# Convolution stage: the copies into column order issued on ScalarE instead of GpSimd, and two tap matrices instead of three in one half of the channels

## The chip, the cores and the metric

The kernel runs on one core of a Trainium2 chip. The metric is the device time of one execution in microseconds, as the median of several executions. Before the change three executions took 19363.97, 19373.8 and 19378.93 us, median 19373.8.

## The reference

The model has four layers on an image of 2 x 128 x 128 pixels with 128 channels in float32. Only the beginning of the last layer matters here:

```python
xz = x @ W_in.T                               # 128 -> 512 channels, x is group-normalised
xc, z = jnp.split(xz, 2, axis=-1)             # 256 channels each
xc = conv_general_dilated(xc, conv_w, (1, 1), ((1, 1), (1, 1)),
                          feature_group_count=256) + conv_b      # 3 x 3, depthwise
xc = silu(xc)
x1 = _local_scan(xc, Hh, Ww, 32, 32)                      # windows of 32 x 32, row order
x2 = _local_scan(xc, Hh, Ww, 32, 32, column_first=True)   # the same windows, column order
x3, x4 = x1 and x2 reversed
# selective scans of x1 .. x4, layer norm, gate with silu(z), output projection
```

So each of the 256 channels is a projection of the 128 inputs, followed by a 3 x 3 filter of its own (nine taps), a bias and a silu. The scans then need every window of 32 x 32 pixels in row order and in column order.

## The kernel before

`program` (L1705) runs the layers one after the other: `layer0`, `layer1`, `layer2`, and for the last layer `layer3_conv` (L1092), `layer3_scan` (L1216) and `layer3_out` (L1624). Between the parts of the last layer the data goes through tensors in DRAM. `layer3_conv` fills `xs` (each window in row order, `xs[0]`, and in column order, `xs[1]`, with channels on the partitions) and `xst` (each window with pixels on the partitions). `layer3_scan` reads them.

`layer3_conv` works on strips of 32 rows: two images (`b`) times four strips (`hg`), eight in all. In each strip:

- `xpad` (two buffers) is the normalised input of 34 rows by 130 columns. It is loaded in pieces `x3l` on SP's queue (L1138) and normalised by ScalarE (L1142); GpSimd clears the border (L1127 to L1132).
- For each half `e` of the 256 channels, TensorE multiplies `xpad` with the projection `win` into `zps` (L1157) and ScalarE copies it to `xz` (L1161, three buffers), whose side columns GpSimd clears (L1152, L1153).
- The strip is cut into four groups `g` of eight rows. A tap of the filter can be computed in two ways. As a matrix, TensorE multiplies `xpad`, shifted by the tap, with `cw`, which is the projection times the tap's weight, and sums the taps in PSUM in `cps` (L1170, two buffers). As a vector operation, VectorE multiplies the shifted `xz` with the weight in `cv` and adds it to `acc` (L1179, three buffers). Its first operation for a group adds to `cps`, the others add to `acc` itself. Taps 0 to 2 (`MAT`) are matrices, taps 3 to 8 (`VEC`) are vector operations, in both halves. So VectorE has six operations of 128 x 1024 per group, 384 in the stage. A matrix costs two matmuls per group, each of which leaves two records in the trace.
- ScalarE applies bias and silu to `acc` and writes `xw` (L1183, three buffers), which holds the four windows of the strip one after the other.
- For each window `wg`, GpSimd copies `xw` in column order to `xv` (L1192, two buffers, one half of the channels per copy): it reads with a step of 32 elements and writes without gaps. SP's queue stores `xw` (L1193) and `xv` (L1196). TensorE transposes `xw` in blocks of 128 x 128 into `xtps` (L1205, two buffers), ScalarE copies these to `xt` (L1210, two buffers), and SP's queue stores it to `xst` (L1213).

[...] In this stage the order isn't written out by hand: a scheduler interleaves the work of neighbouring groups, halves and strips on each engine, within the limits of the buffers and dependencies. In the scan the order is held as written (`in_order`, L114). [...]

Of the kernel before, what the change touches and what calls it, by code (L numbers as in the profile page):

```python
# [9 lines left out]
F32 = mybir.dt.float32  # L10
AF = mybir.ActivationFunctionType
ALU = mybir.AluOpType
# [3 lines left out]
P = 128  # L16
# [6 lines left out]
def cols_of(handle, n, offset=0):  # L23

    return bass.AP(handle.tensor, handle.offset + offset, [[1, P], [P, n // P]])


def rows_of(handle, n, offset=0):

    return bass.AP(handle.tensor, handle.offset + offset, [[0, P], [1, n]])  # L30
# [1061 lines left out]
def layer3_conv(tc, cs, ins, x3, xs, xst, sc, sh):  # L1092

    nc = tc.nc  # L1100
    MAT = (0, 1, 2)
    VEC = (3, 4, 5, 6, 7, 8)
    with ExitStack() as ctx:
        pool = lambda name, bufs, **kw: ctx.enter_context(tc.tile_pool(name=name, bufs=bufs, **kw))
        w = pool("l3a_w", 1)
        two = pool("l3a_two", 2)
        three = pool("l3a_three", 3)
        ps_t = pool("l3a_ps_t", 2, space=PSUM)
        ps_z = pool("l3a_ps_z", 2, space=PSUM)
        ps_c = pool("l3a_ps_c", 2, space=PSUM)  # L1110
        win = w.tile([P, 256], F32, name="win")
        nc.sync.dma_start(win, ins["winT"][:, 0:256])

        cw = w.tile([P, len(MAT), 256], F32, name="cw")
        nc.sync.dma_start(cw.rearrange("p t e -> p (t e)"), rows_of(ins["conv_w_t"], len(MAT) * 256))

        cv = w.tile([P, 9, 2], F32, name="cv")
        nc.sync.dma_start(cv.rearrange("p t e -> p (t e)"), cols_of(ins["conv_w_t"], 9 * 256))
        cb = w.tile([P, 2], F32, name="cb")
        nc.sync.dma_start(cb, cols_of(ins["L3_conv_conv_b"], 256))  # L1120
        nc.vector.tensor_tensor(
            cw, cw, win.unsqueeze(1).to_broadcast([P, len(MAT), 256]), ALU.mult
        )
        for b in range(NB):
            for hg in range(4):
                xpad = two.tile([P, 34, 130], F32, name=f"xpad_{b}_{hg}", tag="xpad")
                nc.gpsimd.memset(xpad[:, :, 0:1], 0.0)  # L1127
                nc.gpsimd.memset(xpad[:, :, 129:130], 0.0)
                if hg == 0:
                    nc.gpsimd.memset(xpad[:, 0:1, 1:129], 0.0)  # L1130
                if hg == 3:
                    nc.gpsimd.memset(xpad[:, 33:34, 1:129], 0.0)  # L1132
                r = max(32 * hg - 1, 0)
                end = min(32 * hg + 33, HW)
                while r < end:
                    n = min(8, end - r)
                    xl = two.tile([P, 8, HW], F32, name=f"x3l_{b}_{hg}_{r}", tag="x3l")
                    nc.sync.dma_start(  # L1138
                        xl[:, 0:n, :].rearrange("c r w -> c (r w)"), x3[b, :, r * HW : (r + n) * HW]
                    )  # L1140
                    p0 = r - 32 * hg + 1
                    nc.scalar.activation(  # L1142
                        xpad[:, p0 : p0 + n, 1:129], xl[:, 0:n, :], AF.Identity,
                        bias=sh[:, b : b + 1], scale=sc[:, b : b + 1],
                    )
                    r += n
                xw = []
                for e in range(2):
                    t = f"{b}_{hg}_{e}"
                    ep = slice(e * P, (e + 1) * P)  # L1150
                    xz = three.tile([P, 34, 130], F32, name=f"xz_{t}", tag="xz")
                    nc.gpsimd.memset(xz[:, :, 0:1], 0.0)  # L1152
                    nc.gpsimd.memset(xz[:, :, 129:130], 0.0)  # L1153
                    for r in range(0, 34, 4):
                        n = min(4, 34 - r)
                        zps = ps_z.tile([P, 4, HW], F32, name=f"zps_{t}_{r}", tag="zps")
                        nc.tensor.matmul(  # L1157
                            zps[:, 0:n, :], win[:, ep], xpad[:, r : r + n, 1:129],
                            start=True, stop=True,
                        )  # L1160
                        nc.scalar.copy(xz[:, r : r + n, 1:129], zps[:, 0:n, :])  # L1161
                    xwe = three.tile([P, 4, 32, 32], F32, name=f"xw_{t}", tag="xw")
                    xw.append(xwe)
                    for g in range(4):
                        cps = ps_c.tile([P, 8, HW], F32, name=f"cps_{t}_{g}", tag="cps")
                        for i, tap in enumerate(MAT):
                            dy, dx = tap // 3, tap % 3
                            for h in range(2):
                                r = 8 * g + 4 * h + dy
                                nc.tensor.matmul(  # L1170
                                    cps[:, 4 * h : 4 * h + 4, :], cw[:, i, ep],
                                    xpad[:, r : r + 4, dx : dx + HW],
                                    start=(i == 0), stop=(i == len(MAT) - 1),
                                )
                        acc = three.tile([P, 8, HW], F32, name=f"acc_{t}_{g}", tag="acc")
                        for i, tap in enumerate(VEC):
                            dy, dx = tap // 3, tap % 3
                            r = 8 * g + dy
                            nc.vector.scalar_tensor_tensor(  # L1179
                                acc, xz[:, r : r + 8, dx : dx + HW], cv[:, tap, e : e + 1],  # L1180
                                cps if i == 0 else acc, ALU.mult, ALU.add,
                            )
                        nc.scalar.activation(  # L1183
                            xwe[:, :, 8 * g : 8 * g + 8, :].rearrange("p g r w -> p r g w"),
                            acc.rearrange("p r (g w) -> p r g w", w=32),
                            AF.Silu, bias=cb[:, e : e + 1],
                        )
                for wg in range(4):
                    t = f"{b}_{hg}_{wg}"
                    xv = two.tile([P, 2, 32, 32], F32, name=f"xv_{t}", tag="xv")  # L1190
                    for e in range(2):
                        nc.gpsimd.tensor_copy(xv[:, e], xw[e][:, wg].rearrange("p h w -> p w h"))  # L1192
                        nc.sync.dma_start(  # L1193
                            xs[0, b, hg, wg, :, e, :], xw[e][:, wg].rearrange("p h w -> p (h w)")
                        )
                        nc.sync.dma_start(  # L1196
                            xs[1, b, hg, wg, :, e, :], xv[:, e].rearrange("p w h -> p (w h)")
                        )
                    xt = two.tile([P, 8, 256], F32, name=f"xt_{t}", tag="xt")
                    for g in range(4):  # L1200
                        tps = ps_t.tile([P, 2, 2, P], F32, name=f"xtps_{t}_{g}", tag="x3t")
                        for j in range(2):
                            for e in range(2):
                                h0 = 4 * (2 * g + j)
                                nc.tensor.transpose(  # L1205
                                    tps[:, j, e, :],
                                    xw[e][:, wg, h0 : h0 + 4, :].rearrange("p h w -> p (h w)"),
                                    cs.ident,
                                )
                        nc.scalar.copy(  # L1210
                            xt[:, 2 * g : 2 * g + 2, :], tps.rearrange("p j e d -> p j (e d)")
                        )
                    nc.sync.dma_start(xst[b, hg, wg].rearrange("(t p) d -> p t d", p=P), xt)  # L1213
# [603 lines left out]
```

## Time and profile before

| what | value |
| --- | --- |
| median of three executions | 19373.8 us |
| the profiled execution, whole | 19390.22 us |
| its span | 19388.3 us |
| convolution: VectorE's first operation of L1179 starts | 6059.55 us |
| its last starts | 6636.2 us |
| first VectorE operation of the scan's preparation | 6674.98 us |
| first operation of the scan itself (L1579) | 6707.10 us |
| VectorE busy over the span | 16402.8 us (85%) |
| ScalarE busy | 14886.8 us (77%) |
| TensorE busy | 14890.7 us (77%) |
| GpSimd busy | 12448.3 us (64%) |

A row of the group view gives the source line, the engine, the operation, the tiles written and read, shape and count, then the busy time in us, the mean duration of one operation in ns, and the engine's idle time just before these operations with what ended it. A row of the timeline gives start and length in us of a run of like operations. In it, a bracket is idle time ahead of the run and what ended it. PE is TensorE's matmul, PEld its weight load, DVE VectorE, ACT ScalarE, POOL GpSimd, SP the engine that issues the DMAs. A table of windows gives for each stretch its length, the busy time of each engine with the count of operations, the clock granted to TensorE, the mean busy share of the DMA engines and GB/s.

Most of the span is the scan, which starts after the convolution. The convolution takes about 3% of it.

### The profile page before, as it was taken

To read this page: it belongs to the slowest core of one execution; us is meant where nothing else is said; L and a number is where in the kernel's file an instruction comes from. 1 tells how busy PE (TensorE), PEld (TensorE's weight loads), DVE (VectorE), ACT (ScalarE), POOL (GpSimd) and SP (SyncE) were. 2 spreads that over 40 slices of the span, in tenths; PEclk is the share of its full clock that TensorE was granted. 3 is DMA by queue.
4 is the path that set the end of the run, shared out by engine and by line. 5 is a ranking of instruction groups with operands and counts; after the bars stand their busy time and mean duration, and the time that the engine had idled before them with its cause. 6 is when DMAs were issued, how large, how long until landed. Compare 5 with 4: busy or idle time off the path is not lost. (4 is left out here: it accounts for less than half of the span.)

```text
span 19388.3 us, 284041 instructions
## 1 busy us (share of the span) xinstructions
PE 14890.7 (77%) x100346; PEld 8797.9 (45%) x100346; DVE 16402.8 (85%) x20891; ACT 14886.8 (77%) x30269; POOL 12448.3 (64%) x6909
## 2 busy tenths in 40 slices
PE   7888888886446777777777777777777777777756
PEld 5665666663113344444444444444444444444445
DVE  6666666336668899999999999999999999999977
ACT  4665666333333499999999999999999999999932
POOL 0000000110001399999999999999999999999954
PEclk9999999887778898999899999999999999999977
DMA  2000000221113444444444444444444444444455
GB/s 48 23 22 22 17 17 14 70 64 50 38 38 118 168 118 113 117 113 117 111 119 115 116 115 116 120 111 120 112 120 111 120 110 121 115 115 116 114 177 182
DMA packets 1302045, 1861.84 MB, mean 96 GB/s; under 512 B 120269, under 2 KB 685517, under 8 KB 1298318
## 3 DMA queue, kind: packets, MB, share of 16 engines
q1 hardware_dynamic: 1264638, 1834.44, 36.1%
q8 instruction: 797, 13.06, 0.3%
q10 hardware_dynamic: 35984, 9.22, 0.2%
q14 instruction: 626, 5.13, 0.1%
HBM read 1398.74 MB, written 444.60 MB: 95 GB/s over the span
## 5 line engine op out<-in xcount | busy, mean ns | idle before, releaser
L1579 DVE TENSOR_TENSOR_SCAN hs<-da,state,ups 128x512 f32<-128x512 f32 x8192 | 9924.2, 1260 | 349.9 <-PE ups L1571 285.0
L1597 POOL TENSOR_TENSOR hs<-hs,cb 128x2048 f32<-128x2048 f32 x2048 | 9389.2, 4585 | 432.0 <-ACT state L1591 185.4
L1571 PE MATMUL ups<-ident,but 128*128 128x128 f32 x32768 | 5595.9, 302 | 2547.1 <-DVE hs L1579 1650.1
L1571 PEld LDWEIGHTS ups<-ident,but 128*128 128x128 f32 x32768 | 3882.8, 151 | 6164.1 <-DVE hs L1579 3512.0
L1536 ACT ACTIVATE but<-du,bt 128x256 f32<-128x256 f32 x12800 | 5330.1, 498 | 4.8 <-DVE du L1434 4.2
L1512 ACT ACTIVATE da<-db,na 128x512 f32<-128x512 f32 x8192 | 5226.5, 711 | 24.3 <-DMA db<-dd 19.9
L1550 PE MATMUL yps<-hs,sel 128*32 128x512 f32 x16384 | 2504.1, 687 | 31.5 <-POOL hs L1597 12.6
L1531 POOL TENSOR_TENSOR but<-du,bt 128x256 f32<-128x256 f32 x3584 | 2161.8, 625 | 17.9 <-issue 17.9
L282 POOL TENSOR_TENSOR xres<-xres,rowb 128x256 f32<-128x256 f32 x128 | 93.4, 730 | 2645.4 <-DMA xres<-in_x 2536.3
L390 ACT COPY pT<-tps 128x512 f32<-128x512 f32 x1280 | 724.6, 587 | 1121.0 <-PE tps L385 1121.0
L385 PE MATMUL tps<-ident,s 128*128 128x128 f32 x8192 | 1179.6, 283 | 367.9 <-DVE pT L388 273.4
L358 DVE CUSTOM_DVE_ANT_0 s<-sps,relbias 128x512 f32<-128x512 f32 x2048 | 1321.3, 683 | 113.5 <-PE sps L342 108.0
L385 PEld LDWEIGHTS tps<-ident,s 128*128 128x128 f32 x8192 | 888.0, 142 | 898.4 <-issue 485.6
L370 ACT ACTIVATE s<-s,nm 128x1024 f32<-128x1024 f32 x1024 | 1163.5, 1137 | 85.0 <-DVE nm L368 81.6
L1127 POOL MEMSET xpad<- 128x34 f32 x8 | 1.3, 165 | 1577.8 <-PE xs L1021 1503.0
L342 PE MATMUL sps<-kc,qT 32*128 32x512 f32 x4096 | 595.0, 648 | 0.8 <-DVE nm L358 0.8
L1591 ACT COPY state<-hs 128x4 f32<-128x4 f32 x2048 | 381.1, 186 | 264.3 <-DVE hs L1579 264.3
L388 DVE COPY pT<-tps 128x512 f32<-128x512 f32 x768 | 526.8, 686 | 55.2 <-PE tps L385 54.6
L1317 PE MATMUL xdps<-xc,xpw 128*40 128x512 f32 x1024 | 541.7, 611 | 15.0 <-DMA xpw<-in_x_projT 15.0
L1349 PE MATMUL dtps<-xd,dtw 65*128 65x512 f32 x1024 | 549.5, 619 | 0.0
L1550 PEld LDWEIGHTS yps<-hs,sel 128*32 128x32 f32 x16384 | 340.5, 114 | 459.3 <-issue 306.8
L725 POOL TENSOR_TENSOR xr<-xr,row_ln_b 128x512 f32<-128x512 f32 x64 | 81.3, 1271 | 706.9 <-DMA xr<-x 470.8
(290 smaller groups left out, 18402.1 us busy)
## 6 DMA issues: line engine op xcount, KB each, us to landing
db<-dd SPq DMA_DIRECT2D x1024, 512.0 KB
cb<-cd SPq DMA_DIRECT2D x1024, 256.0 KB
xc<-xs SPq DMA_DIRECT2D x256, 512.0 KB
dd<-dl SPq DMA_DIRECT2D x256, 512.0 KB
ys<-yt SPq DMA_DIRECT2D x256, 512.0 KB
yl<-ys SPq DMA_DIRECT2D x256, 512.0 KB
ut<-xst SPq DMA_DIRECT2D x128, 512.0 KB
ut<-xst SPq DMA_DIRECT2D x512, 128.0 KB
```

What stands on the lines that cost most here:

```text
L342: nc.tensor.matmul(sps, v["qT"][hp, qt * P : (qt + 1) * P], kc[b, wh + g][hp, :, c0 : c0 + 32], start=True, stop=True,)
L358: nc.vector.tensor_tensor_reduce(v["s", qt][:, h, cols], v["sps", qt, g][h], bias[:, qt, h, cols], op0=ALU.add, op1=ALU.min, scale=-1.0, s ...
L370: nc.scalar.activation(s[:, h, :], s[:, h, :], AF.Exp, bias=nm[:, 2, h : h + 1], scale=-1.0, accum_out=v["sums"][:, qt, h : h + 1],)
L385: nc.tensor.transpose(tps[:, j, :], v["s", qt][:, h, k0 : k0 + P], cs.ident)
L390: nc.scalar.copy(dst, tps)
L1512: nc.scalar.activation(da[:, j, :], held[i]["db"][:, 4 * e + j, :], AF.Exp, scale=na[:, k, c : c + 1])
L1531: nc.gpsimd.tensor_tensor(but[:, j, :, n, :], du[:, tb], bt[:, tb, c : c + 1].unsqueeze(2).to_broadcast([P, 8, 32]), ALU.mult,)
L1536: nc.scalar.activation(but[:, j, :, n, :], du[:, tb], AF.Copy, scale=bt[:, tb, c : c + 1])
L1550: nc.tensor.matmul(v["yps"][e][32 * j : 32 * j + 32, :], sel, hs[:, j, :], start=(q == 0), stop=(q == 3),)
L1571: nc.tensor.transpose(ups[:, tb * P : (tb + 1) * P], v[("but", q, tb // 2)][:, tb % 2, 4 * e + j].rearrange("p n c -> p (n c)"), cs.ident,)
L1579: nc.vector.tensor_tensor_scan(o, a, u, state[:, c0 + j : c0 + j + 1], ALU.mult, ALU.add)
L1597: nc.gpsimd.tensor_tensor(hs, hs, v["cb"][:, s // 2, :].unsqueeze(1).to_broadcast([P, 4, T]), ALU.mult)
```

## The change

The copies into column order move from GpSimd to ScalarE. The number of taps that are matrices now depends on the half of the channels: three in half 0, as before, and two in half 1, where VectorE gets the third one (tap 2) as a seventh operation per group. `cw` keeps room for three taps. In the diff, `MATS[e]` takes the place of the lists `MAT` and `VEC`; the rest follows from it.

```diff
-    MAT = (0, 1, 2)
-    VEC = (3, 4, 5, 6, 7, 8)
+
+    MATS, TAPS = (3, 2), 9
+    most = max(MATS)
...
-        cw = w.tile([P, len(MAT), 256], F32, name="cw")
-        nc.sync.dma_start(cw.rearrange("p t e -> p (t e)"), rows_of(ins["conv_w_t"], len(MAT) * 256))
+        cw = w.tile([P, most, 256], F32, name="cw")
+        nc.sync.dma_start(cw.rearrange("p t e -> p (t e)"), rows_of(ins["conv_w_t"], most * 256))
...
-            cw, cw, win.unsqueeze(1).to_broadcast([P, len(MAT), 256]), ALU.mult
+            cw, cw, win.unsqueeze(1).to_broadcast([P, most, 256]), ALU.mult
...
-                        for i, tap in enumerate(MAT):
+                        for tap in range(MATS[e]):
                             dy, dx = tap // 3, tap % 3
                             for h in range(2):
                                 r = 8 * g + 4 * h + dy
                                 nc.tensor.matmul(
-                                    cps[:, 4 * h : 4 * h + 4, :], cw[:, i, ep],
+                                    cps[:, 4 * h : 4 * h + 4, :], cw[:, tap, ep],
                                     xpad[:, r : r + 4, dx : dx + HW],
-                                    start=(i == 0), stop=(i == len(MAT) - 1),
+                                    start=(tap == 0), stop=(tap == MATS[e] - 1),
                                 )
                         acc = three.tile([P, 8, HW], F32, name=f"acc_{t}_{g}", tag="acc")
-                        for i, tap in enumerate(VEC):
+                        for tap in range(MATS[e], TAPS):
                             dy, dx = tap // 3, tap % 3
                             r = 8 * g + dy
                             nc.vector.scalar_tensor_tensor(
                                 acc, xz[:, r : r + 8, dx : dx + HW], cv[:, tap, e : e + 1],
-                                cps if i == 0 else acc, ALU.mult, ALU.add,
+                                cps if tap == MATS[e] else acc, ALU.mult, ALU.add,
                             )
...
                     for e in range(2):
-                        nc.gpsimd.tensor_copy(xv[:, e], xw[e][:, wg].rearrange("p h w -> p w h"))
+                        nc.scalar.copy(xv[:, e], xw[e][:, wg].rearrange("p h w -> p w h"))
```

## The prediction

> **What bounds the kernel now.** The page's 40 slices place the convolution in the 13th and 14th slice only. I then read its groups of instructions (window 6020 to 6680 us), the view of line L1179, the timelines of VectorE, GpSimd and TensorE, the ScalarE groups kept apart by shape, and the busy table of the stage's end. The groups first (count, then busy us and mean ns, then idle before it):
>
> ```profile
> L1179 DVE SCALAR_TENSOR_TENSOR acc<-xz,cv,acc 128x1024 f32<-128x1024 f32 x320 | 462.0, 1472 | 7.3
> L1170 PE MATMUL cps<-xpad,cw 128*128 128x512 f32 x768 | 353.6, 602 | 0.9 <-DVE acc L1179 0.9
> L1192 POOL COPY xv<-xw 128x1024 f32<-128x1024 f32 x64 | 154.7, 2454 | 106.5 <-ACT xw L1183 92.7 <-issue 8.3 <-DMA xs<-xv 3.6
> L1179 DVE SCALAR_TENSOR_TENSOR acc<-xz,cv,cps 128x1024 f32<-128x1024 f32 x64 | 81.6, 1275 | 49.6 <-PE cps L1170 34.9 <-POOL xv L1192 13.3 <-ACT xw L1183 1.4
> ```
>
> VectorE works from 6059.55 to 6637.5 us (last start 6636.2 plus 1.28): 577.9 us, almost without a pause, so it sets the stage. But 320 of its operations have a mean of 1472 ns, and the view of L1179 gives minimum, median and maximum:
>
> ```profile
> L1179 DVE SCALAR_TENSOR_TENSOR acc<-xz,cv,acc x320: 1271/1284/3106, 6060.9 to 6636.2; 128x1024 f32<-128x1024 f32 x160
> ```
>
> A few are very long. VectorE's timeline beside GpSimd's shows which:
>
> ```profile
> 6490.66 1.28 DVE L1179 SCALAR_TENSOR_TENSOR acc<-xz,cv,cps 128x1024 f32<-128x1024 f32 x1 [1.42 <-ACT xw L1183]
> 6491.97 13.12 DVE L1179 SCALAR_TENSOR_TENSOR acc<-xz,cv,acc 128x1024 f32<-128x1024 f32 x5
> 6515.01 5.25 DVE L1179 SCALAR_TENSOR_TENSOR acc<-xz,cv,acc 128x1024 f32<-128x1024 f32 x4
> 6532.45 1.28 DVE L1179 SCALAR_TENSOR_TENSOR acc<-xz,cv,cps 128x1024 f32<-128x1024 f32 x1 [3.33 <-POOL xv L1192]
> 6545.16 7.25 DVE L1179 SCALAR_TENSOR_TENSOR acc<-xz,cv,acc 128x1024 f32<-128x1024 f32 x6
> 6490.49 16.44 POOL L1192 COPY xv<-xw 128x1024 f32<-128x1024 f32 x6 [0.96 <-ACT xw L1183]
> ```
>
> While six copies run on GpSimd (16.44 us), five VectorE operations take 13.12 us; elsewhere six take 7.25. Two start-to-start distances also show. In the 7.25 us row two acc tiles alternate: (7.25 - 1.28) / 5 = 1.195 us. In the 5.25 us row each operation reads what the one before it wrote: (5.25 - 1.28) / 3 = 1.32 us. By the instruction order of the kernel before, 174 of 384 operations follow one on the same acc, 210 don't. So 577.9 = 210 x 1.195 + 174 x 1.32 (480.6) + stalls 33.5 (49.6 less the first wait of 16.1, which precedes 6059.55) + a rest of 63.8. The rest is the collision with the copies; the excess of mean over median, 320 x 0.188 = 60, agrees.
>
> TensorE is close behind:
>
> ```profile
> 6383.79 17.33 PE L1170 MATMUL cps<-xpad,cw 128*128 128x512 f32 x40
> ...
> 6433.35 1.97 PE L1205 MATMUL xtps<-ident,xw 128*128 128x128 f32 x8 [7.95 <-ACT xt L1210]
> ```
>
> ```profile
> 6385.80:6459.00 73.20, 65.16 (x197) 31.74 (x196) 67.98 (x48) 31.46 (x47) 20.69 (x14) 0.95 0.56 203
> ```
>
> A matmul of L1170 is two records of 17.33 / 40 = 0.43 us. In one strip of 73.2 us (last row: length, then busy PE, PEld, DVE, ACT, POOL) TensorE is busy 65.2 and waits some 8 for ScalarE. ScalarE is busy 31.5.
>
> [...] operations on xz and acc (both SBUF) reach 3106 ns, those with cps in PSUM stay at 1275. [...] The copy reads with a step of 128 bytes; on GpSimd its shortest takes 1912 ns. [...]
>
> **The change, part by part.**
> *GpSimd.* All 64 copies (154.7 us busy) leave. With them go the 63.8 us of collision and the 13.3 us that VectorE waited for them. GpSimd keeps the memsets of L1127 to L1153, which nothing now delays.
> *VectorE.* Half e=0 keeps 3 matrices and 6 vector taps. Half e=1 has 2 and 7: 32 more operations, x 1.195 = 38.2 us on the path.
> *The order.* In the built order of the changed kernel 410 of 416 operations alternate between two acc tiles, across strip boundaries too; 6 don't. VectorE's work is 410 x 1.195 + 6 x 1.32 = 497.9 us, against 480.6 + 63.8 before. The better alternation alone is worth 168 x 0.125 = 21 us.
> *TensorE.* 64 matmuls, 128 records, fall away: 128 x 0.43 = 55 us, 6.9 per strip, leaving 58.3 of work against VectorE's 497.9 / 8 = 62.2. cw keeps its three matrices, so its load and multiply stay.
> *ScalarE.* It gets 64 copies. No row shows it reading with this step. Its rows that write with a large step, and one without:
>
> ```profile
> L687 ACT COPY acc<-ips 128x512 f32<-128x512 f32 x64 | 61.8, 1025 | 13.8 <-PE ips L683 13.8
> L1210 ACT COPY xt<-xtps 128x512 f32<-128x512 f32 x128 | 72.1, 586 | 62.8 <-PE xtps L1205 47.7 <-DMA xst<-xt 14.0 <-ACT xt L1210 0.8
> L1022 ACT COPY xh<-xs 128x1024 f32<-128x1024 f32 x32 | 32.4, 1012 | 310.3 <-PE xs L1021 310.3
> ```
>
> 512 elements take 586 ns in order and 1025 with a step. So a copy of 1024 lies between 1.01 us and about 2.05; I take 1.85, near GpSimd's 1.91 for the same pattern. Eight per strip make 14.8; ScalarE goes from 31.5 to 46 of 62 us. That is covered as long as the wait in its queue is. A copy waits until the store of its xv buffer (two) has landed, and the silu of L1183 queues behind it, which frees acc (three buffers). I follow the order on ScalarE from T, the last VectorE operation of a strip: silu 1.15, xz 0.5, copy 1.85 (T+3.5); its store lands about 4.5 later (6122.94 us: the first of two copies took 2.45, and GpSimd got on at 6129.89); two copies, T+11.7; silu of the next strip's first group, T+12.9. VectorE needs that buffer for the strip's fourth group, 13 operations after T: T+15.5. Next: four xt copies, two more copies, second silu at T+20.4, needed 20 operations after T, at T+23.9. Slack 2.6 and 3.5 us, so the copies and this wait cost nothing on the path at the price taken. TensorE's transposes wait for ScalarE's xt copies too, but followed the same way the products for groups 3, 4, 5 are done by T+4, T+9.3, T+17 and wanted at T+9.6, T+15.5, T+23.9.
> *SP.* The order of its DMA issues is unchanged.
> *Residual stalls.* Of 33.5 us, 13.3 go with the copies. Of the 18.8 for cps I leave 1 us per strip: 8 (bounds 0 and 30).
> *The end.* From 6644 to 6668 the DMA engines are full:
>
> ```profile
> 6650.00:6655.00 5.00, 2.78 (x17) 2.12 (x16) 0.00 (x0) 2.09 (x5) 3.82 (x2) 0.84 1.05 372
> 6660.00:6668.00 8.00, 0.00 (x0) 0.00 (x0) 0.00 (x0) 0.00 (x0) 0.00 (x0) 0.50 1.01 345
> ```
>
> (the last two columns are DMA share and GB/s.) The bytes stay, but ScalarE now does six xv copies in line with 12 xt copies after the last silu, 6 x 1.85 + 12 x 0.5 = 17 us plus waits for stores, where it took 16.3 with its waits before (6639.8 to 6656.1); the last store starts later into an emptier queue. I take +3 (bounds -2 and +10).
>
> **Sum.** 577.9 - 497.9 = 80 saved, less 8 of stalls, less 3 at the end: 69. The scan and all else keep their instructions. The profiled execution took 19390.2 us (span 19388.3), so 19321; it lay 16.4 above the median of the three runs, 19373.8, so the median becomes about 19305.
>
> **Rivals.**
> *TensorE sets the pace.* It keeps its wait of about 8 us per strip and sheds only its 6.9: 73.2 - 6.9 = 66.3 x 8 = 530, 48 saved less 3: 19329. For: its idle gaps bring back slow matmuls (after the gap above, two records took 1.60 us where 1.02 is usual). Against: the leads of 5.6 to 6.9 us worked out above.
> *ScalarE's queue takes back half.* With copies of 2.05 and stores that land in 11 us rather than 4.5, T+12.9 becomes 1.7 + 2.05 + 11 + 4.1 + 1.15 = T+20, 4.5 late; 8 strips lose 36, which leaves 33: 19341, no measurable change. Against: GpSimd waited only 3.6 us in all for these stores.
> *ScalarE becomes the bound, slower than before.* If a copy costs c, the second silu is ready at T + 11.15 + 5c, wanted at T+23.9. The gain per strip is 69 / 8 = 8.6, so it turns into a loss from c = 4.3 us; at 5 us the stall is 12.2 per strip, 3.6 over the gain, 29 in all: 19403. For: no row shows this read pattern on ScalarE. Against: it is over twice any row of 1024 elements.
>
> **How the numbers follow.** Forecast 0.64, TensorE 0.18, half taken back 0.12, slower 0.06. 0.2%, about what a measurement can tell, is 39 us, so faster begins below 19335. Within the forecast the bounds give 19292 (no stalls, end -2) to 19334 (stalls 30, end +10); with 4 us for the rounding of the distances (416 x 0.01), TensorE's case and the half-way one it becomes 19288 to 19347. Faster: 0.64 and most of 0.18, 0.79; same 0.15; slower 0.06.
>
> **What would show it.** Right: L1179 with 352 + 64 operations, mean of the acc form about 1285 and maximum near the minimum; VectorE from first to last operation near 506 us; the copies on ScalarE at 1.0 to 2.05 us; strips of 63 us. Wrong: VectorE idle for ScalarE xw (buffer acc), for PE cps over 2 us per strip, copies over 2.5 us, long L1179 operations without GpSimd, or an end longer than 40 us from VectorE's last operation to the first of the scan's.

## The result, and the profile after

The changed kernel took 19298.72 us, median of six executions (19287.09 to 19332.67), against 19373.31 (19356.78 to 19389.06) for six of the kernel before: ratio 0.9965, 95% interval 0.9952 to 0.9978. It is faster, by 74.6 us; the forecast was 19305.

The profiled execution of the changed kernel took 19287.09 us (span 19285.3), 103.1 us less than that of the kernel before, but only 73.4 of these belong to the convolution. Both executions can be cut at the same marks:

| part | before | after | difference |
| --- | --- | --- | --- |
| up to VectorE's first filter operation | 6059.55 | 6054.44 | -5.1 |
| filter operations, first start to last end | 577.9 | 504.5 | -73.4 |
| from there to the first operation of the scan | 69.6 | 68.5 | -1.1 |
| scan, first to last start of the scan's VectorE line | 11780.5 | 11753.8 | -26.7 |
| from there to the end of the span | 900.7 | 904.0 | +3.3 |

The scan has the same instructions in both. In these two profiled executions and those of the experiments below it took 11730.8 to 11780.5 us whatever was done to the convolution, so its 26.7 us are variation, and single whole times can't be read to better than some 25 us either way (two matrices in both halves, below, has a longer stage than the changed kernel and about its whole time, with the shortest scan of all). The stage is therefore judged by the second row, which I call the stage below.

The groups of instructions of the changed kernel (count, busy us and mean ns, then idle before them), shapes kept apart; most lines of this stage stand one further down than in the kernel before. I call an operation that adds to `acc` the acc form (both its large inputs are in SBUF), and the first one of a group, which adds to `cps` in PSUM, the cps form.

```profile
L1180 DVE SCALAR_TENSOR_TENSOR acc<-xz,cv,acc 128x1024 f32<-128x1024 f32 x352 | 426.6, 1278 | 0.3
L1171 PE MATMUL cps<-xpad,cw 128*128 128x512 f32 x640 | 294.6, 596 | 3.1 <-DVE acc L1180 3.1
L1193 ACT COPY xv<-xw 128x1024 f32<-128x1024 f32 x64 | 127.4, 2036 | 0.4 <-DMA xs<-xv 0.3
L1180 DVE SCALAR_TENSOR_TENSOR acc<-xz,cv,cps 128x1024 f32<-128x1024 f32 x64 | 81.6, 1275 | 21.4 <-PE cps L1171 17.4 <-ACT xw L1184 3.8
```

The view of line L1180 (minimum, median and maximum in ns, then first and last start):

```profile
L1180 DVE SCALAR_TENSOR_TENSOR acc<-xz,cv,acc x352: 1275/1279/1285, 6055.8 to 6557.7; 128x1024 f32<-128x1024 f32 x176
```

The mean of the acc form fell from 1472 to 1278 ns and its maximum from 3106 to 1285: no filter operation is stretched any more. VectorE does 32 operations more and is 73 us sooner done. Its waits for `cps` (17.4 us) and for `xw` (3.8 us) come to 21.2 us; 16.1 of them are the first wait, ahead of the stage, and 5.1 are left inside: 1.3 for `cps` and 3.8 for `xw`.

How close the other engines are shows in a table of two windows inside the stage (length, then busy us of PE, PEld, DVE, ACT and POOL, clock, DMA share, GB/s):

```profile
6249.00:6309.00 60.00, 56.37 (x171) 25.70 (x170) 57.71 (x49) 45.06 (x53) 0.45 (x4) 1.00 0.69 248
6309.00:6369.00 60.00, 56.12 (x176) 25.75 (x174) 59.71 (x51) 46.03 (x55) 0.68 (x6) 1.00 0.69 247
```

VectorE is busy 58 to 60 of 60 us, TensorE 56, ScalarE 45 to 46.

The first of these windows holds a strip's end. Two rows of VectorE's and seven of ScalarE's timeline there (start, length, and in brackets the idle time ahead and its end):

```profile
6241.64 1.28 DVE L1180 SCALAR_TENSOR_TENSOR acc<-xz,cv,cps 128x1024 f32<-128x1024 f32 x1
6263.52 1.28 DVE L1180 SCALAR_TENSOR_TENSOR acc<-xz,cv,cps 128x1024 f32<-128x1024 f32 x1 [1.48 <-ACT xw L1184]
6250.76 0.58 ACT L1211 COPY xt<-xtps 128x512 f32<-128x512 f32 x1 [0.75 <-PE xtps L1206]
6251.24 1.15 ACT L1184 ACTIVATE xw<-acc,cb 128x1024 f32<-128x1024 f32 x1
6252.76 2.05 ACT L1193 COPY xv<-xw 128x1024 f32<-128x1024 f32 x1
6255.19 2.03 ACT L1193 COPY xv<-xw 128x1024 f32<-128x1024 f32 x1
6258.49 3.94 ACT L1193 COPY xv<-xw 128x1024 f32<-128x1024 f32 x2 [0.29 <-DMA xs<-xv]
6262.33 1.16 ACT L1184 ACTIVATE xw<-acc,cb 128x1024 f32<-128x1024 f32 x1
6269.57 1.24 ACT L1184 ACTIVATE xw<-acc,cb 128x1024 f32<-128x1024 f32 x1
```

By the instruction order, 6241.64 is the next strip's first group and the old strip's last operation stands three places behind it, so it ends at 6241.64 + 3 x 1.195 + 1.28 = 6246.5: the T of the prediction. The silu of that last group starts only at 6251.24, 4.7 us later, because it stands in ScalarE's queue behind four xt copies that wait for TensorE's transposes (they start at 6246.77, 6248.10, 6249.43 and 6250.76, each after 0.64 to 0.75 us of waiting). Then come four copies, and the silu that frees the buffer for the strip's fourth group ends at 6263.49 = T+17.0. VectorE wanted it at T+15.5 and waits 1.5 us. The second silu ends at 6270.81 = T+24.3, against T+23.9 wanted; VectorE, late by then, doesn't wait for it.

### The profile page after: what moved, and what is told of

It is laid out like the page before. It is cut to its first block, busy times and chain, and to the rows that moved or that the text cites. A ratio compares the mean times of both kernels' runs of the same rounds, so it can differ in the third digit from the quotient of the medians.

```text
span 19285.3 us, 283793 instructions
## 1 busy us (share of the span) xinstructions
PE 14812.1 (77%) x100218; PEld 8743.6 (45%) x100218; DVE 16359.1 (85%) x20923; ACT 14999.0 (78%) x30333; POOL 12306.5 (64%) x6845
## 5 line engine op out<-in xcount | busy, mean ns | idle before, releaser
L1513 ACT ACTIVATE da<-db,na 128x512 f32<-128x512 f32 x8192 | 5227.4, 711 | 23.9 <-DMA db<-dd 20.7
```

The source lines that it names most:

```text
L1513: nc.scalar.activation(da[:, j, :], held[i]["db"][:, 4 * e + j, :], AF.Exp, scale=na[:, k, c : c + 1])
```

## The experiments

Each is the changed kernel with one edit; where work is added it is unread, and nothing that is computed changes, except in the one that says so. "Same-acc" counts operations that follow one on the same acc in the instruction order. The traces agree where waits and collisions don't hide the distances: 174, 352 and 4 operations start 1.25 to 1.4 us after the one ahead in "copies on ScalarE, three matrices in both halves", "written order" and "two matrices in both halves". The last column has the kernel before as it ran beside each experiment (median, and number of executions). Its single executions lay between 19344.65 and 19411.93 us, so whole times compare only within a row. Six experiments ran once (reads, writes, written order, each copy twice, two matrices in both halves, copies in order); they are judged by their stage alone.

| experiment | stage, us | same-acc of all | whole time, us | before beside it, us |
| --- | --- | --- | --- | --- |
| before | 577.9 | 174 of 384 | 19373.31 | |
| changed | 504.5 | 6 of 416 | 19298.72 | 19373.31 (6) |
| copies on ScalarE, three matrices in both halves | 523.8 | 174 of 384 | 19324.22 | 19373.62 (19) |
| copies on GpSimd, three and two matrices | 578.7 | 6 of 416 | 19361.61 | 19373.62 (19) |
| changed, GpSimd reads beside it | 575.5 | 6 of 416 | 19361.03 | 19373.62 (19) |
| changed, GpSimd writes beside it | 504.5 | 6 of 416 | 19294.92 | 19344.65 (1) |
| changed, filter operations in written order | 541.9 | 352 of 416 | 19341.28 | 19373.62 (19) |
| changed, each copy twice | 604.4 | 12 of 416 | 19402.12 | 19344.65 (1) |
| two matrices in both halves | 536.1 | 4 of 448 | 19293.94 | 19344.65 (1) |
| changed, copies read in order | 498.1 | 6 of 416 | 19316.8 | 19397.21 (9) |
| three matrices in half 1's last two groups | 507.1 | 32 of 400 | 19313.97 | 19397.21 (9) |
| three matrices in half 1's last group | 520.6 | 10 of 408 | 19327.45 | 19397.21 (9) |

### One half of the change at a time

```diff
-    MATS, TAPS = (3, 2), 9
+    MATS, TAPS = (3, 3), 9
```

> Copies on ScalarE as in the changed kernel, but three matrices in both halves as before. Stage = VectorE's first to last operation of the taps, 577.9 us before and 504.5 in the changed kernel. VectorE's order has 174 operations behind one on the same acc, as before, so its work is 210 x 1.195 + 174 x 1.32 = 480.6 us. Theory (collision gone, but TensorE keeps 65.2 us of work per strip and waits of its own): at least 8 x 65.2 = 522, some 530 to 550, VectorE waiting for cps; whole time 28 to 48 under before. Rival (the collision is all, and the moved tap only adds 38 us of work): about 480.6 + 15 = 495 to 505, as fast as the changed kernel or faster.

Measured 523.8 us; whole time 19324.22, ratio to before 0.9972 (0.9962 to 0.9983). The copies' move alone brings 54 of the 73 us; the stage lies just over the bound of 522 and under the 530 to 550 that I had expected. VectorE's waits in it, and a window (columns as above):

```profile
DVE acc L1180 <- PE cps L1171: 51.0, 20, 15.8
DVE acc L1180 <- ACT xv L1193: 3.3, 1, 3.3
DVE acc L1180 <- ACT xw L1184: 1.5, 1, 1.5
```

```profile
6249.00:6309.00 60.00, 57.73 (x179) 27.73 (x179) 53.12 (x43) 39.31 (x47) 0.69 (x6) 1.00 0.64 234
```

Without the first wait of 15.8, VectorE waits 35.2 us for cps, in 19 places; in the changed kernel it is 1.3. TensorE is busy 57.7 of 60 us, VectorE 53. So the rival of the prediction, TensorE setting the pace, is real with three matrices in both halves; the sum 480.6 of VectorE's work plus 40.0 of waits gives 520.6 of the 523.8. The order of VectorE's operations is that of the kernel before: the better alternation doesn't come from moving the copies.

The other half alone:

```diff
-                        nc.scalar.copy(xv[:, e], xw[e][:, wg].rearrange("p h w -> p w h"))
+                        nc.gpsimd.tensor_copy(xv[:, e], xw[e][:, wg].rearrange("p h w -> p w h"))
```

> Three and two matrices as in the changed kernel, but the copies stay on GpSimd. VectorE's order has only 6 operations behind one on the same acc, so its work is 497.9 us. Theory (the collision costs what it did before, 64 us, plus waits for the copies): stage 565 to 585, whole time equal to before within 0.2%; operations on acc reach 3 us again. Rival (TensorE's relief and the better order are the gain): stage 505 to 520, whole time 55 us or more under before.

Measured 578.7 us; ratio to before 0.9993 (0.9985 to 1.0002), no measurable change. The long operations are back, as the view of L1180 shows:

```profile
L1180 DVE SCALAR_TENSOR_TENSOR acc<-xz,cv,acc x352: 1270/1274/3027, 6062.4 to 6638.5; 128x1024 f32<-128x1024 f32 x176
```

VectorE has no wait inside the stage here, and the good alternation, so all above 497.9 is collision: 578.7 - 497.9 = 81. The halves don't add up: -54 and +1 alone, -73 together. With the copies on GpSimd, two matrices in half 1 do take away the 33.5 us of waits, but VectorE's own work grows by 17.3 (480.6 to 497.9) and the collision by 17 (63.8 to 81), 34 us together. With the copies on ScalarE the same step takes away 35 us of waits (40.0 to 5.1) for the same 17.3 of work, and there is no collision that could grow.

### What it is about GpSimd that costs

Into the changed kernel I put back GpSimd's reads, with the result in a tile that nobody reads:

```diff
+                        nc.gpsimd.tensor_copy(xd, xw[e][:, wg].rearrange("p h w -> p w h"))
```

> The changed kernel, and GpSimd also makes each of the 64 copies, into a tile that nobody reads. Theory (a GpSimd instruction that reads SBUF stops VectorE operations with two SBUF inputs): operations on acc beside a copy take 2 to 3 us, the stage grows by about 64 us to 560 to 580. Rival (the gain came from elsewhere, a copy on GpSimd is harmless): stage 504 to 510.

and, in another kernel, only writes, which fill a similar time in all:

```diff
+                        for _ in range(2):
+                            nc.gpsimd.memset(xd, 0.0)
```

> The changed kernel, and GpSimd clears a tile of 128 x 1024 twice where e3 copies once; nobody reads it. These instructions write SBUF and read nothing. Theory (only GpSimd's reads collide): operations on acc stay at 1.28 us, stage 504 to 510. Rival (any GpSimd access to SBUF beside them slows them): operations of 2 us and more, stage above 530.

With reads the stage took 575.5 us, 71 more. VectorE's and GpSimd's timelines there:

```profile
6509.77 10.61 DVE L1180 SCALAR_TENSOR_TENSOR acc<-xz,cv,acc 128x1024 f32<-128x1024 f32 x4
6520.30 1.27 DVE L1180 SCALAR_TENSOR_TENSOR acc<-xz,cv,cps 128x1024 f32<-128x1024 f32 x1
6533.87 4.86 DVE L1180 SCALAR_TENSOR_TENSOR acc<-xz,cv,acc 128x1024 f32<-128x1024 f32 x4
6502.12 25.96 POOL L1195 COPY xd<-xw 128x1024 f32<-128x1024 f32 x7 [2.74 <-ACT xw L1184]
```

Four operations take 10.61 us while GpSimd copies, 4.86 when it doesn't; the cps form, with one input in PSUM, stays at 1.27 in the middle of it (1.281 at most in the stage, where the acc form reaches 3.102). With writes alone the stage is 504.5 us to the tenth, as in the changed kernel. These writes wait for nothing, so they don't spread over the stage: they run almost back to back from 6044.2 to 6175.3, the last 108 us of it inside the stage. GpSimd's line, and a window in which it is busy for 52 of 60 us and VectorE without a gap:

```profile
L1196 POOL MEMSET xd<- x128: 951/952/966, 6044.2 to 6174.3; 128x1024 f32 x128
6120.00:6180.00 60.00, 55.89 (x172) 25.67 (x171) 60.00 (x51) 43.77 (x54) 52.31 (x62) 1.00 0.63 232
```

VectorE's line: no operation is longer than 1286 ns.

```profile
L1180 DVE SCALAR_TENSOR_TENSOR acc<-xz,cv,acc x352: 1271/1279/1286, 6068.7 to 6570.6; 128x1024 f32<-128x1024 f32 x176
```

So GpSimd being busy was not enough, nor was its writing: with copies, which read SBUF and write it, the acc form, with two inputs in SBUF, reached 3.10 us, with memsets, which only write, 1.286. Of the two it is the reading that goes with the collision. The step of GpSimd's read was not varied.

The trace with reads also shows how the two get in each other's way. The first copies of the row of seven, one by one, and VectorE's operations beside them:

```profile
6502.12 8.37 POOL L1195 COPY xd<-xw 128x1024 f32<-128x1024 f32 x1 [2.74 <-ACT xw L1184]
6510.55 2.88 POOL L1195 COPY xd<-xw 128x1024 f32<-128x1024 f32 x1
6501.40 7.26 DVE L1180 SCALAR_TENSOR_TENSOR acc<-xz,cv,acc 128x1024 f32<-128x1024 f32 x6
6508.57 1.27 DVE L1180 SCALAR_TENSOR_TENSOR acc<-xz,cv,cps 128x1024 f32<-128x1024 f32 x1
6509.77 1.82 DVE L1180 SCALAR_TENSOR_TENSOR acc<-xz,cv,acc 128x1024 f32<-128x1024 f32 x1
6511.51 3.01 DVE L1180 SCALAR_TENSOR_TENSOR acc<-xz,cv,acc 128x1024 f32<-128x1024 f32 x1
```

The first copy lasts 8.37 us, while six acc-form operations run at their normal distance; it ends at 6510.49, 1.92 us after the cps-form operation has started, and the shortest copy of the kernel before took 1.91. The acc-form operation of 6509.77 ends at 6511.59, 1.10 us after that copy; the second copy ends at 6513.43, 1.84 us after that operation; the next operation ends at 6514.52, 1.09 us after the second copy. So the two take turns here by whole instructions. All three traces show it: in the kernel before, in the one with only the taps changed and in this one, all 50, 58 and 57 operations longer than 1.4 us end 1.07 to 1.10 us after a copy has ended. What they take beyond 1.275 us sums to 61, 80 and 77 us, about what the sums of VectorE's work and waits leave over: 63.8, 81 and 78.

### What the alternation is worth

VectorE's filter operations were tied together in the order in which they are written, without added waits between engines:

```diff
+    chain = []
...
+                            now = nc.cur_bb.bb.instructions[-1]
+                            if chain:
+                                tc.add_manual_dep(
+                                    now, chain[-1].name,
+                                    mybir.DependencyInfo(mybir.DependencyClass.NoSync, mybir.DependencyReason.DATA),
+                                    reason="one_chain",
+                                )
+                            chain.append(now)
```

> The changed kernel with VectorE's tap operations held in program order, group after group: 352 of 416 follow one on the same acc. Theory (1.32 us from start to start behind one on the same acc, 1.195 otherwise): 352 x 1.32 + 64 x 1.195 = 541 us of work, stage 541 to 550. Rival (the distance does not depend on it, and the 1.32 came from something else): 416 x 1.195 = 497, stage 500 to 510.

Measured 541.9 us: 37 more for the same operations, none of them stretched. A row of VectorE's timeline:

```profile
6250.78 7.89 DVE L1181 SCALAR_TENSOR_TENSOR acc<-xz,cv,acc 128x1024 f32<-128x1024 f32 x6
```

Six operations on one acc take 7.89 us, so (7.89 - 1.285) / 5 = 1.32 from start to start, where six that alternate take 7.26. 352 x 1.32 + 64 x 1.195 = 541.1, within 1 us of the stage. The duration of one operation is the same (median 1285 ns); only the distance shows it.

### How much room ScalarE's queue has

```diff
-                        nc.scalar.copy(xv[:, e], xw[e][:, wg].rearrange("p h w -> p w h"))
+                        for _ in range(2):
+                            nc.scalar.copy(xv[:, e], xw[e][:, wg].rearrange("p h w -> p w h"))
```

> The changed kernel with every copy into column order made twice on ScalarE, so a copy costs c = 4.07 us in its queue instead of 2.04. Theory (the slack worked out in the prediction: the second silu of the next strip is ready at T + 11.15 + 5c = T + 31.5 and wanted at T + 23.9): 7.6 us lost per strip, stage 504.5 + 61 = 565, VectorE waiting for ScalarE (xw), ScalarE busy 59 us or more per strip. Rival (ScalarE's queue has more room than that): stage 504 to 520.

Measured 604.4 us, 100 more and not 61: the direction was right and the size short by 39. VectorE's waits first; the 17.1 us ahead of the stage are among them. Ten of the 128 copies have no record in this trace, which may be why part of the waits has no releaser ("issue"):

```profile
DVE acc L1180 <- issue: 49.8, 4, 13.1
DVE acc L1180 <- ACT xw L1184: 46.9, 8, 14.0
DVE acc L1180 <- PE cps L1171: 23.8, 8, 17.1
```

A strip's end on ScalarE, and the VectorE operation that waits:

```profile
6287.48 1.15 ACT L1184 ACTIVATE xw<-acc,cb 128x1024 f32<-128x1024 f32 x1
6298.11 1.17 ACT L1184 ACTIVATE xw<-acc,cb 128x1024 f32<-128x1024 f32 x1
6300.98 7.71 ACT L1194 COPY xv<-xw 128x1024 f32<-128x1024 f32 x4
6309.03 7.55 ACT L1194 COPY xv<-xw 128x1024 f32<-128x1024 f32 x4
6317.38 1.23 ACT L1184 ACTIVATE xw<-acc,cb 128x1024 f32<-128x1024 f32 x1
6318.69 1.28 DVE L1180 SCALAR_TENSOR_TENSOR acc<-xz,cv,cps 128x1024 f32<-128x1024 f32 x1 [10.71 <-issue]
```

The operation starts 0.08 us after the silu of 6317.38 has ended (6318.61): the wait is for ScalarE. Between the silu of 6287.48 and this one stand twelve single copies, six of them extra. 6 x 2.04 = 12.2 us per strip, and the stage lost 99.9 / 8 = 12.5 on average: all that was added between these two silus arrives, so the queue had next to no slack. (The other two extra copies of a strip, of eight, stand elsewhere.) I had given it 3.5 us and counted five copies, since one was thought to lie inside a wait for a store.

The reverse, copies that cost half: they read each window in row order here, so the reordering is left out of this kernel.

```diff
-                        nc.scalar.copy(xv[:, e], xw[e][:, wg].rearrange("p h w -> p w h"))
+                        nc.scalar.copy(xv[:, e], xw[e][:, wg])
```

> The changed kernel, but the copies on ScalarE read each window in row order, without the step of 32 elements (so xs[1] holds row order here: the reordering is left out). Theory: a copy costs 2.04 us because of the step it reads with; without it the mean falls to 1.0 to 1.05 us, like the row of L1022. VectorE sets the stage either way, so the stage stays at 501 to 504.5 us, and VectorE's waits for ScalarE's xw fall from 3.8 us towards 0. Rival: ScalarE is slowed by its neighbours in this stage, and the copy stays near 2 us; or ScalarE's share of the stage was worth more than its visible waits, and the stage falls below 498.

The copies' line:

```profile
L1193 ACT COPY xv<-xw x64: 1040/1049/1089, 6103.5 to 6582.1; 128x1024 f32<-128x1024 f32 x64
```

1.05 us against 2.04: the step of the read is half of a copy's cost. VectorE waits for nothing inside the stage, which takes 498.1 us, 3 below what I had expected at least and on the 497.9 of VectorE's operations alone. That is all but the rival's "below 498": ScalarE's part was worth more than the 3.8 us of waits for it that can be seen. So in the changed kernel 6.4 of 504.5 us are left to be had from everything that isn't VectorE's own work: the 5.1 of visible waits and a rest of 1.3.

### Where the matrices should be

```diff
-    MATS, TAPS = (3, 2), 9
+    MATS, TAPS = (2, 2), 9
```

> The changed kernel with two matrices in both halves: 448 operations on VectorE, 4 of them behind one on the same acc: 444 x 1.195 + 4 x 1.32 = 535.9 us. Theory (VectorE alone sets the changed kernel's stage): 536 to 545. Rival (TensorE still holds VectorE back in the changed kernel): under 525.

Measured 536.1 us, and VectorE, in the view of L1180, without any wait but the first one:

```profile
L1180 DVE SCALAR_TENSOR_TENSOR acc<-xz,cv,acc x384: 1265/1270/1285, 6055.3 to 6588.8; 128x1024 f32<-128x1024 f32 x192
  PE cps L1171: 14.7, 1
```

444 x 1.195 + 4 x 1.32 = 535.9. VectorE alone sets this one: 32 operations more cost 31.6 us against the changed kernel. With (3, 3) at 523.8, held by TensorE, and (2, 2) at 536.1, held by VectorE, (3, 2) at 504.5 is below both. I tried the two points between (3, 2) and (3, 3), in search of a faster version:

```diff
-                        for tap in range(MATS[e]):
+                        mats = 3 if e == 0 or g >= 2 else 2
+                        for tap in range(mats):
```

and `mats` for `MATS[e]` in the lines below; the second one has `g >= 3`.

> The changed kernel with three matrices also in half 1, but only in its last two groups of each strip: 400 VectorE operations, of which 32 follow one on the same acc. If VectorE still sets the stage: 368 x 1.195 + 32 x 1.32 = 482 us, with the 6.6 that the changed kernel has above its own sum (504.5 - 497.9) about 489. TensorE gets 3.4 us more per strip (8 records of 0.43), about 62 against VectorE's 60, so theory: it begins to hold VectorE back, waits for PE cps of 1 to 3 us per strip, stage 490 to 505. Whole time within 0.1% of the changed kernel.

> The same with three matrices in half 1 only in the last group of each strip: 408 operations, 10 of them on the same acc: 398 x 1.195 + 10 x 1.32 = 489, plus 6.6: 495 if VectorE sets the stage. TensorE gets 1.7 us more per strip, about 60.5 against VectorE's 61. Theory: this is near the balance of the two, stage 494 to 500; rival: the TensorE bound seen with three matrices everywhere already holds here, stage over 504. Whole time within 0.1% of the changed kernel.

Neither is faster by what can be measured. The first took 507.1 us, 2 over the range I had given (whole time 19313.97, ratio to before 0.9956, 0.9941 to 0.9970, which is the changed kernel's own within its interval): VectorE's work is 482 us, but the waits for cps have come, 22.5 us in 19 places besides the first:

```profile
DVE acc L1181 <- PE cps L1172: 37.2, 20, 14.7
```

The second took 520.6 us (ratio 0.9963, 0.9951 to 0.9976). That is over the rival's 504, but not by the rival's cause: TensorE hardly holds it back, ScalarE does. Its waits, and ScalarE's timeline:

```profile
DVE acc L1181 <- ACT xw L1185: 28.5, 10, 4.5
DVE acc L1181 <- PE cps L1172: 17.7, 2, 17.3
```

```profile
6256.35 3.97 ACT L1194 COPY xv<-xw 128x1024 f32<-128x1024 f32 x2
6262.52 3.90 ACT L1194 COPY xv<-xw 128x1024 f32<-128x1024 f32 x2
6266.32 2.18 ACT L1185 ACTIVATE xw<-acc,cb 128x1024 f32<-128x1024 f32 x2
```

Here the scheduler put both silus behind all the copies of the strip; in the changed kernel the first of the two stands ahead of the last pair of copies. VectorE waits for them ten times, up to 4.5 us. VectorE's own work is 9 us less than in the changed kernel (489), its waits for `xw` 25 us more. So with little slack on ScalarE an edit of the taps can cost more through the queue's order than it saves in work; the order by itself was not varied. I found no version that beats the changed kernel by what can be measured.

## Why the prediction was right, and what was mis-sized

The forecast was that VectorE sets the stage, that its collision with GpSimd's copies goes, and that the extra operations cost less than the alternation and the collision give: 69 us saved. The case came in, at 74.6 us in the medians and 73.4 in the stage. By its steps:

- *Collision (63.8).* Right, and shown twice over: put back by reads alone it takes 78 us over VectorE's 497.9, by the old copies 81. That it is larger there than in the kernel before fits the 33.5 us in which VectorE stood still in the kernel before and couldn't collide; no run shows this apart.
- *38.2 us more VectorE work, alternation worth 21.* Right. Two matrices in both halves cost 31.6 more, the written order 37.4 more, both within 1 us of counts times 1.195 and 1.32. The alternation belongs to the taps' half of the change, not to the copies': (3, 3) has the old order. I took it from the instruction order without saying which edit brings it.
- *TensorE (55 us shed, work of 58.3 per strip).* Right in effect: cps waits inside the stage are 1.3 us. That (3, 3) has 35.2 shows that this part of the change was needed for the full gain. The rival "TensorE sets the pace" was real for the copies alone and is removed by the taps.
- *Residual stalls (8).* 5.1, of which 3.8 are for ScalarE and not for cps, so the size was close and the cause was not.
- *A copy on ScalarE (1.85 us).* 2.04, at the upper bound of 2.05, which was twice a copy in order. The read with a step cost 1.99 ns an element (2036 / 1024), about as the write with a step of L687, 2.00 (1025 / 512).
- *Slack of ScalarE's queue (2.6 and 3.5 us).* The term most out. The silu at the strip's end was taken to start at T; it started 4.7 us later, behind four xt copies that wait for transposes. The slack was -1.5 and not 2.6 at the strip shown. It cost little because the miss was little; doubling the copies showed that nothing was in reserve. That the copies cost next to nothing on the path was therefore in part luck: the slack that was to pay for it wasn't there.
- *Wait for stores.* ScalarE waited 0.3 us in all for them. I had them on the path at 4.5 us per strip; by the time a buffer was wanted again its store had landed.
- *The end (+3).* 0: from VectorE's last filter operation to its first of the scan's preparation it is 37.5 us in both kernels, all of it a wait for the landing of one load (`na`). ScalarE's longer row of copies ends in the changed kernel while the DMA engines are still full, as a table of the end shows (last columns: DMA share and GB/s); they are full to 6590, at a share of 1.01 to 1.04 from 6565 on, and in the kernel before at 1.01 to 1.05 from 6645 to 6668. So I put the 37.5 down to the bytes. With copies at half the cost the distance is 36.5 us, little less; with every copy made twice it is 43.5, and only there does ScalarE's row lengthen it. The table:

```profile
6575.00:6580.00 5.00, 1.65 (x8) 1.18 (x8) 0.00 (x0) 4.32 (x7) 0.00 (x0) 0.80 1.01 380
6580.00:6585.00 5.00, 0.00 (x0) 0.00 (x0) 0.00 (x0) 1.17 (x1) 0.00 (x0) 0.50 1.04 391
```

- *The rival on the other side, a loss from copies of 4.3 us.* At twice 2.04 the stage is at 604.4, 26 us over the kernel before: slower already below 4.3, so the price given there was too high. With six copies in line and no slack, the gain of 73.4 / 8 = 9.2 per strip would be used up at about 2.04 + 9.2 / 6 = 3.6 us (an estimate from these runs). Its chance was small because the price was bounded by 2.05; that held.

Against the sum, 2.9 us came from fewer stalls and 3 from the end, and 1.5 went to a rest in the stage that no view shows (504.5 - 497.9 - 5.1): together the 4.4 us between 69 and 73.4.

## What to carry to other kernels

If a few operations of a group last twice its minimum or more (here 3.1 us against 1.27), look for what runs beside them on GpSimd before counting operations; here moving the reader away was worth more (54 us alone) than the work that came in exchange, and the other half of the change did nothing until it had happened. In a stage with three engines busy 45 to 60 of 60 us, don't take the idle share of an engine for slack (ScalarE had a quarter idle and nothing in reserve): work out the slack from what stands ahead in the queue, the waits of the instructions ahead included (here four xt copies put a silu off by 4.7 us). And read distances between starts, not durations, when deciding whether dependent operations should be interleaved (here 1.32 us against 1.195, at durations of 1.285 and 1.279).

## What the runs showed of the hardware

- A 128 x 1024 float32 copy on ScalarE that read with a step of 128 bytes took 2.04 us (mean of 64), in order 1.05 (median of 64).
- GpSimd's copies and VectorE operations with two inputs in SBUF took turns by whole instructions: side by side they alternated, and a VectorE operation of 1.27 us lasted up to 3.1. All 165 operations longer than 1.4 us, in three traces, ended 1.07 to 1.10 us after a copy had ended. Both lost. At the 1.91 us of the shortest copy, GpSimd's 64 would take 64 x 1.91 = 122 us (an estimate from the kernel before); put back, they took 181 themselves and cost VectorE 71 us of the stage, about 0.58 for a microsecond of copying at that shortest time.
- Some copies beside such operations lasted far longer and ended with an operation of the cps form. With reads put back three copies lasted 7.0 to 8.4 us, with only the taps changed four lasted 7.1 to 8.6. The operations beside them kept their length until then, and each of the seven copies ended 1.91 to 1.94 us after the start of a cps-form operation. Why these waited so long, while others alternated with the acc form, was not tried.
- GpSimd's memsets of 128 x 1024 (0.95 us each, 108 of their 122 us inside the stage) cost the same VectorE operations nothing: 504.5 us with and without.
